# A selective-scan and window-attention kernel: counting who waits for a tile's room in the order's ranks, and taking two norms out of PSUM early

## The chip, the cores and the metric

The kernel runs on one core of a Trainium2 chip. The metric is the device time of one execution in microseconds (us). Five instruction queues are at work: PE (TensorE, matrix products), DVE (VectorE), ACT (ScalarE), POOL (GpSimd) and SP (SyncE, which here issues nearly all DMAs). Every queue works in order: an instruction that waits holds up all behind it on its engine.

## The reference

The input x is (8, 192, 64, 64), all in fp32. Two layers follow each other.

Layer 0 projects the 192 channels to 384, convolves each channel with a 3x3 kernel, and scans the image in four directions. For each direction and channel three gates Gl, Gm, Gr and the factors L, U, D come from a 16-wide projection of the pixel; the gates are divided by the sum of their absolute values. Columns are cut into chunks of 8, and in each chunk a step t does

```python
s = jnp.abs(Gl) + jnp.abs(Gm) + jnp.abs(Gr) + eps
hn = l * x + gl * h_up + gm * h + gr * h_dn      # h_up, h_dn: the rows above and below
out = out * Us + xs * Ds
```

The four directions are summed, normalised over channels, scaled by a global response norm per image, and projected back to 192 channels.

Layer 1 is a transformer block over windows of 8x8 pixels: a layer norm (the "first norm" here), q, k and v for six heads of 32, q and k brought to unit length, scores kept where they are among the 16 largest of a row, a softmax with a position bias, the product with v, a projection, a second norm, a GELU layer of width 768, and two residual sums. In the parts that matter here:

```python
shortcut = _layer_norm(xs, norm1_g, norm1_b)     # rsqrt(var + 1e-5) * g + b
attn = jnp.einsum('bhnd,bhmd->bhnm', _l2n(q), _l2n(k)) * temperature
```

## The kernel before

Three kinds of work are written down for each image b, as generators of steps.

`front` (line 490) does the first projection and the convolution and writes the result to DRAM twice, in the two orders in which the scans read it. `scan` (line 608) does the eight steps t. In each, for four directions and three blocks of 128 channels (12 tiles), PE makes the gates at line 673 into PSUM: two gates and L into three banks "g" and one bank "nb" (`gates`); later, for each pair of tiles, four more banks "g" with D and U (`both`). DVE, ACT and POOL do the rest: ab (L730, L761), pr (L737, L739, L776, L780, L791), rr (L772, L774), nb (L769, L787, L795), the new state hid (L802), and the output's parts dx and hu (L828, L833). `window_row` (line 1004) takes one row of eight windows (512 pixels, four tiles of 128 tokens) through all of layer 1: 64 rows in all.

PSUM has eight banks. Two are kept for "nb" (pool `n_ps`), and six are shared by everything else: pool `l_ps`, tag "lp", both for the "g" tiles of the scan and for the "lp" tiles of front, norms and windows (`bank()`, line 466). PE can't begin a tile before its bank has been read for the last time by whoever read the tile before.

In `window_row` the first norm goes like this. For each half t2 of the row, PE makes two token tiles of 192 columns side by side in one bank pz (L1047). The weights are centred, so the mean is zero already. ACT squares each from PSUM with an accumulated sum (L1053; the squares themselves land in the SBUF tile s0 and are overwritten later). POOL, ACT and POOL make the reciprocal root ss (`rsqrt`, L478 to L485). Then DVE multiplies the bank by ss and by the norm's gain n1_g into s0 (L1069), the last reader of pz. s0 is transposed by PE (L1012) and copied to sT (L1020).

For q and k, PE makes 384 columns in a bank pq (L1093), ACT copies them to the SBUF tile qk (L1101), then squares them in place in PSUM (L1108), and DVE sums the squares over each head (L1115), the last reader of pq. A reciprocal root follows, and DVE scales qk (L1166).

The order of the instructions on all queues is written by the program itself. Each step is given to `Plan` (line 78) with an engine, an assumed cost, its reads and writes, and a lane (steps of one lane that make tiles of one tag keep their order among themselves). A `Held` object is a tile that is to be made: the first step that uses it takes a slot of its pool, and the slot comes free when the last user has ended. `run` (line 170) plays the steps through: on each engine, of the steps that can start, it takes first those that need not wait longer than SLACK, and among them the one of the lowest rank. `order` (line 146) plays twelve times. The first time the ranks are those of the images; after each play, a step's rank becomes the latest time at which it could have started so that none of its successors would start later:

```python
for s in run:
    s.rank = min([d.start for d in s.after], default=s.end) - (s.end - s.start)
```

The shortest of the twelve plays is the order that is emitted. A step counts as successor only if it depends on the data or comes later on the same tile; a step that takes the slot which this one sets free isn't counted.

Of the kernel before, what the change touches and what calls it, by code (L numbers as in the profile page):

```python
# [25 lines left out]
AF = mybir.ActivationFunctionType  # L26
ALU = mybir.AluOpType
# [4 lines left out]
P = 128  # L32
# [22 lines left out]
class Held:  # L55


    def __init__(self, pool, shape, name, bufs=None, tag=None, dtype=F32):
        self.args = pool, shape, dtype, name, tag or name, bufs or pool.bufs
        self.tag, self.bufs = (id(pool), tag or name), bufs or pool.bufs  # L60
        self.users, self.left, self.end, self.tile = [], 0, 0.0, None

    def make(self):
        pool, shape, dtype, name, tag, bufs = self.args
# [13 lines left out]
class Plan:  # L78
# [67 lines left out]
    def order(self):  # L146

        before = [s.before for s in self.steps]
        tiles = {h: h.left for s in self.steps for h in s.held}
        best = None
        for _ in range(self.RUNS):
            for s, k in zip(self.steps, before):
                s.before, s.ready = k, 0.0
            for h, k in tiles.items():
                h.left, h.end = k, 0.0
            run = self.run()  # L160
            if best is None or self.length < best[0]:
                best = self.length, run, [s.start for s in run]
            for s in run:
                s.rank = min([d.start for d in s.after], default=s.end) - (s.end - s.start)
        self.length, run, starts = best
        for s, t in zip(run, starts):
            s.start = t
        return run

    def run(self):  # L170

        slots, queues = {}, {}
        counted, full = {}, {}
        done = []

        def clock(k):
            if k not in full:
                full[k] = counted.get(k - 1, 0.0) >= self.ENTRY
            return 2.4 if full[k] else 1.2

        def stream(t, cycles, share):
            while cycles > 1e-6:
                k = int(t / self.TICK)
                rate = clock(k)
                m = min(cycles, ((k + 1) * self.TICK - t) * rate + 1e-3)
                counted[k] = counted.get(k, 0.0) + m * share
                cycles -= m
                t += m / rate
            return t


        for s in self.steps:
            for h in s.makes:
                queues.setdefault((h.tag, s.lane), []).append(s)
                slots.setdefault(h.tag, [0.0] * h.bufs)
        first = {k: 0 for k in queues}

        def startable(s):

            t, need = s.ready, {}  # L200
            for h in s.makes:
                q = queues[h.tag, s.lane]
                if q[first[h.tag, s.lane]] is not s:
                    return None
                need[h.tag] = need.get(h.tag, 0) + 1
            for tag, n in need.items():
                kept = 0
                if s.lane and (tag, 0) in queues and first[tag, 0] < len(queues[tag, 0]):

                    f = queues[tag, 0][first[tag, 0]]  # L210
                    if not f.before and all(slots[h.tag] for h in f.makes if h.tag != tag):
                        kept = sum(h.tag == tag for h in f.makes)
                if len(slots[tag]) < n + kept:
                    return None
                t = max(t, sorted(slots[tag])[n + kept - 1])
            return t

        engines = sorted({s.engine for s in self.steps})
        pool = {e: [] for e in engines}
        dirty = set(engines)  # L220
        for s in self.steps:
            if not s.before:
                pool[s.engine].append(s)
        free = {e: 0.0 for e in engines}
        todo = len(self.steps)
        best = {e: None for e in engines}
        while todo:
            for e in dirty:
                pick = None
                for s in pool[e]:  # L230
                    t = startable(s)
                    if t is None:
                        continue
                    t = max(t, free[e])
                    late = max(0.0, t - free[e])
                    key = (late > self.SLACK, late if late > self.SLACK else 0.0, s.rank, s.n)
                    if pick is None or key < pick[0]:
                        pick = key, t, s
                best[e] = pick
            dirty = set()  # L240
            e = min((x for x in engines if best[x]), key=lambda x: best[x][1])
            _, t, s = best[e]
            s.start = t
            if e == "PE":
                cycles, share = s.cost
                end = stream(t + 60.0, cycles, share)
                free[e], s.end = end, end + 140.0
            else:
                hold, more = s.cost
                free[e] = t + hold  # L250
                s.end = free[e] + more
            pool[e].remove(s)
            dirty.add(e)
            todo -= 1
            done.append(s)
            for h in s.makes:
                first[h.tag, s.lane] += 1
                slots[h.tag].remove(min(slots[h.tag]))
            touched = bool(s.makes)
            for h in s.held:  # L260
                h.left -= 1
                h.end = max(h.end, s.end)
                if not h.left:
                    slots[h.tag].append(h.end + self.HOP)
                    touched = True
            if touched:
                dirty.update(engines)
            for d in s.after:
                d.before -= 1
                d.ready = max(d.ready, s.end + (self.HOP if d.engine != e else 30.0))  # L270
                if not d.before:
                    pool[d.engine].append(d)
                    dirty.update(engines)
        self.length = max(s.end for s in done)
        return sorted(done, key=lambda s: (s.start, s.n))
# [8 lines left out]
def tile_ss2d_then_window_attention(ctx: ExitStack, tc: tile.TileContext, a: dict, out: bass.AP):  # L284
# [719 lines left out]
    def window_row(b, g, z, sc, bb):  # L1004
# [31 lines left out]
        for t2 in range(2):  # L1036
            pz = bank()
            ss = Held(small, [P, 2], "ss")
            for k in range(2):

                def tokens(t2=t2, k=k, pz=pz):
                    tt = 2 * t2 + k
                    for ct in range(CT):
                        for w in range(2):
                            half = pz()[64 * w : 64 * w + 64, k * DM : (k + 1) * DM]
                            tok = view(zg(), [[CH, 64]], ct * 512 + 2 * tt + w)
                            nc.tensor.matmul(half, lhsT=tok, rhs=w_out[:, ct, :], start=ct == 0, stop=ct == CT - 1)  # L1047

                plan("PE", mm(3, DM), tokens, r=[zg], w=[(pz, k), (s0, "room")])
                plan(  # L1050
                    "ACT",
                    (430.0, 100.0),
                    lambda k=k, pz=pz, ss=ss, t2=t2: nc.scalar.activation(  # L1053
                        s0()[:, 2 * t2 + k, :], pz()[:, k * DM : (k + 1) * DM], AF.Square, accum_out=ss()[:, k : k + 1]
                    ),
                    r=[(pz, k)],
                    w=[(s0, t2), (ss, k)],
                )
            plan(
                "POOL",  # L1060
                tiny,
# [2 lines left out]
            )  # L1064
            rsqrt(ss, ss, [P, 2], "ss")

            def scaled(t2=t2, pz=pz, ss=ss):
                for k in range(2):
                    nc.vector.scalar_tensor_tensor(  # L1069
                        s0()[:, 2 * t2 + k, :],  # L1070
                        pz()[:, k * DM : (k + 1) * DM],
                        ss()[:, k : k + 1],
                        n1_g,
                        ALU.mult,
                        ALU.mult,
                    )

            plan("DVE", (650.0, 90.0), scaled, r=[pz, ss], w=[(s0, t2)])
            yield
        plan.lane = 7  # L1080
        two_blocks(sT, "sT", s0)
# [5 lines left out]
        for tt in range(NT):  # L1087
            pq = bank()

            def projected(tt=tt, pq=pq):  # L1090
                tok = slice(tt * P, (tt + 1) * P)
                for ci in range(2):
# [9 lines left out]
                r=[pq],  # L1102
                w=[(qk, tt)],
            )
            plan(
                "ACT",
                act(DIN),
                lambda pq=pq: nc.scalar.activation(pq()[:, 0:DIN], pq()[:, 0:DIN], AF.Square),  # L1108
                r=[(qk, tt)],
                w=[pq],  # L1110
            )
            plan(
                "DVE",
                vec(DIN),
                lambda tt=tt, pq=pq: nc.vector.tensor_reduce(  # L1115
                    nn()[:, tt, :], pq()[:, 0:DIN].rearrange("p (h d) -> p h d", d=HD), AX.X, ALU.add
                ),
                r=[pq],
                w=[(nn, tt)],
            )  # L1120
            yield
# [500 lines left out]
```

## Time and profile before

| what | value |
|---|---|
| median of 3 runs | 8548.28 us (8543.92 to 8550.57) |
| the profiled execution's own time | 8535.73 us |
| its span, first to last instruction | 8533.9 us |
| mean granted TensorE clock | 0.818 |
| PE matmuls ahead of the first window row's start (0 to 1180 us) | 844.7 us busy |
| rows beside scans (1180 to 7936 us) | 5728.3 us busy |
| rows alone after the last gate matmuls (7936 to 8534 us) | 493.2 us busy |

In the lines of the profile, L1069 is line 1069 of the kernel before. "out<-in" names the tiles written and read, and "32x512 f32" their partitions and elements. Busy time is the time in which the group had an instruction under way; mean is one instruction's own time, so neighbours that overlap have more mean than busy time. The idle time before a group is that of its engine, with what ended it: when that is the reader of a PSUM bank, and the group is a matmul whose inputs had long been there, the matmul waited for the bank's room. An fp32 matmul of the program appears as two in the profile in most forms. Idle time of an engine costs nothing where it isn't on the chain that ends last.

### The profile page before, as it was taken

The numbers are of one execution on the slowest core, as the hardware profiler recorded it, in microseconds if no ns is written. First come the engines' busy times: TensorE is split into PE (matmuls) and PEld (weight loads), VectorE is DVE, ScalarE is ACT, GpSimd is POOL, SyncE is SP. The second block draws the span as 40 slices with busy tenths as digits, with TensorE's granted clock in tenths as the row PEclk, the third lists the DMA queues.
The fourth block names the chain that finished last, engine by engine and source line by source line (L and its number), as shares of the span: only waits on it lengthen the run. The fifth ranks groups of instructions, "written<-read, shape, count | busy, mean of one in ns | idle before, by whom it ended". The sixth has DMA issues, their size and how long they took to land.

```text
span 8533.9 us, 147117 instructions
## 1 busy us (share of the span) xinstructions
PE 7066.1 (83%) x51224; PEld 3646.0 (43%) x51224; DVE 6350.5 (74%) x15549; ACT 5425.1 (64%) x12281; POOL 5839.1 (68%) x5918
## 2 busy tenths in 40 slices
PE   5787688888888888788888888888888888888887
PEld 2333344444444444444444444444444444444554
DVE  1366778888787887877788777787788888888543
ACT  1354447676676757665676656766577656667776
POOL 0377877778777677777777667676777777777311
PEclk8887578887888889786888888977778878778888
DMA  6776154212533155213531134311211111111110
GB/s 176 188 194 160 49 137 120 79 43 72 137 98 78 36 138 133 70 47 85 147 95 51 42 88 132 107 39 46 56 44 41 46 52 53 40 41 42 26 23 12
DMA packets 1037949, 695.69 MB, mean 82 GB/s; under 512 B 704116, under 2 KB 860215, under 8 KB 1037207
## 3 DMA queue, kind: packets, MB, share of 16 engines
q1 hardware_dynamic: 1035830, 684.99, 30.1%
q8 instruction: 406, 6.65, 0.3%
q14 instruction: 337, 2.75, 0.1%
q10 hardware_dynamic: 1376, 1.30, 0.1%
HBM read 453.43 MB, written 232.67 MB: 80 GB/s over the span
## 4 chain that ended last, share of the span: by engine, by line
PE 37%; DVE 17%; ACT 17%; POOL 13%; DMA 9%; issue 5%; SPq 1%; POOLq 0%; DVEq 0%; ACTq 0%
PE g L673 10%; PE lp L560 4%; PE lp L1477 4%; PE lp L1443 3%; POOL pr L791 3%; DMA strip<-pad 3%; DMA zg<-z 3%; ACT at L1276 2%; PE lp L1093 2%; PE lp L1047 2%; ACT at L1288 2%; POOL ab L761 2%; POOL pr L776 2%; POOL dx L842 2%; DVE pr L737 2%
## 5 line engine op out<-in xcount | busy, mean ns | idle before, releaser
L673 PE MATMUL g<-xe,w_g 32*128 32x512 f32 x3648 | 1301.1, 780 | 316.3 <-DVE dx L828 115.5
L673 PE MATMUL g<-xo,w_g 32*128 32x512 f32 x3648 | 1263.1, 774 | 238.5 <-DVE dx L828 65.1
L761 POOL TENSOR_TENSOR ab<-ab 128x512 f32<-128x512 f32 x672 | 863.2, 1285 | 407.3 <-ACT ab L730 401.4
L791 POOL TENSOR_TENSOR pr<-pr,rr 128x512 f32<-128x512 f32 x672 | 873.0, 1299 | 340.9 <-ACT rr L774 307.0
L776 POOL TENSOR_TENSOR pr<-pr 128x512 f32<-128x512 f32 x672 | 872.9, 1299 | 316.5 <-DVE pr L737 204.5
L730 ACT ACTIVATE ab<-g 128x512 f32<-128x512 f32 x1344 | 770.8, 593 | 320.6 <-PE nb L673 166.2
L560 PE MATMUL lp<-strip,w_cv 128*32 128x256 f32 x9216 | 687.2, 442 | 288.4 <-DMA strip<-pad 264.5
L780 POOL TENSOR_TENSOR pr<-pr 128x512 f32<-128x512 f32 x672 | 869.9, 1295 | 24.3
L842 POOL TENSOR_TENSOR dx<-dx,hu 128x512 f32<-128x512 f32 x576 | 739.0, 1291 | 183.6 <-DVE hu L833 172.3
L673 PEld LDWEIGHTS g<-xe,w_g 32*128 32x128 f32 x3648 | 461.1, 220 | 895.4 <-DVE dx L828 242.5
L673 PEld LDWEIGHTS g<-xo,w_g 32*128 32x128 f32 x3648 | 441.8, 219 | 804.5 <-issue 202.7
L772 ACT ACTIVATE rr<-nb,eps 128x512 f32<-128x512 f32 x672 | 460.0, 685 | 486.5 <-DVE nb L769 423.9
L787 DVE SCALAR_TENSOR_TENSOR nb<-nb,rr 128x512 f32<-128x512 f32 x672 | 465.2, 692 | 338.5 <-ACT rr L774 337.2
L1477 PE MATMUL lp<-hd,w_f 128*64 128x256 f32 (+1 forms) x2304 | 603.9, 500 | 75.2 <-ACT hd L1463 61.0
L795 DVE SCALAR_TENSOR_TENSOR nb<-nb,pr 128x512 f32<-128x512 f32 x672 | 464.8, 692 | 195.6 <-POOL pr L791 191.8
L560 PEld LDWEIGHTS lp<-strip,w_cv 128*32 128x32 f32 x9216 | 314.0, 123 | 669.3 <-issue 357.6
L850 POOL TENSOR_TENSOR y<-y,dx 128x512 f32<-128x512 f32 x384 | 596.4, 1561 | 3.1
L769 DVE TENSOR_TENSOR nb<-nb,ab 128x512 f32<-128x512 f32 x672 | 465.2, 692 | 154.9 <-POOL ab L761 125.8
L752 ACT ACTIVATE nb<-nb 128x512 f32<-128x512 f32 x672 | 396.8, 591 | 221.5 <-DVE pr L737 111.3
L840 POOL TENSOR_TENSOR y<-hu,dx 128x512 f32<-128x512 f32 x192 | 248.8, 1303 | 406.6 <-DVE hu L833 406.2
L833 DVE TENSOR_TENSOR hu<-g,hid 128x512 f32<-128x512 f32 x768 | 519.9, 678 | 8.0 <-PE g L673 6.4
L673 PE MATMUL nb<-xe,w_g 32*128 32x512 f32 x672 | 497.9, 829 | 8.0 <-DVE hid L802 7.9
(201 smaller groups left out, 17042.9 us busy)
## 6 DMA issues: line engine op xcount, KB each, us to landing
strip<-pad SPq DMA_DIRECT2D x1152, 132.0 KB
xd<-xsT SPq DMA_DIRECT2D x384, 256.0 KB
pad<-xin SPq DMA_DIRECT2D x192, 264.0 KB
xs<-st SPq DMA_DIRECT2D x192, 256.0 KB
xsT<-sn SPq DMA_DIRECT2D x192, 256.0 KB
xd<-xs SPq DMA_DIRECT2D x192, 256.0 KB
x<-xs SPq DMA_DIRECT2D x64, 768.0 KB
z<-y SPq DMA_DIRECT2D x64, 768.0 KB
```

What stands on the lines that cost most here:

```text
L560: nc.tensor.matmul(pc()[q * RG : (q + 1) * RG, k * 256 : (k + 1) * 256].rearrange("p (h w) -> p h w", h=4), lhsT=w_cv[:, ct, q, dx, :], rh ...
L673: nc.tensor.matmul(dst, lhsT=w[rows, col : col + P], rhs=xp[rows, :], start=True, stop=True)
L730: lambda r=r: nc.scalar.activation(ab()[:, r, :], g[r](), AF.Abs),
L761: plan("POOL", gp(512), lambda: nc.gpsimd.tensor_add(ab()[:, 0, :], ab()[:, 0, :], ab()[:, 1, :]), w=[ab])
L769: plan("DVE", vec(512), lambda: nc.vector.tensor_add(nb(), nb(), ab()[:, 0, :]), r=[ab], w=[nb])
L776: plan("POOL", gp(512), lambda: nc.gpsimd.tensor_add(one(), one(), pr()[:, 1, :]), r=[(pr, 1)], w=[(pr, 0)])
L780: lambda: nc.gpsimd.tensor_add(one(), one(), pr()[:, 2, :]),
L791: plan("POOL", gp(512), lambda: nc.gpsimd.tensor_mul(one(), one(), rr()), r=[rr], w=[(pr, 0)])
L833: lambda: nc.vector.tensor_mul(like(hu(), d), like(pu(), d), state(d, ct)),
L842: plan("POOL", gp(512), lambda: nc.gpsimd.tensor_add(dx(), dx(), hu()), r=[hu], w=[dx])
L850: nc.gpsimd.tensor_add(y, y, dx().rearrange("p (c i) -> p i c", c=CH))
L1477: nc.tensor.matmul(dst[:, at : at + rhs.shape[-1]], lhsT=lhsT, rhs=rhs, **flags)
```

## The change

It has three parts.

1. In the plan, a slot of a pool now remembers which tile it held. When a step takes the slot, the tile that held it notes this step as `next`. A step's rank is then also bounded by the start of the `next` of each tile that it uses. Among slots that are free equally early, the order in which they are taken is settled by a second number, no longer left open.
2. First norm: DVE multiplies both token tiles by the gain n1_g from pz into s0 in one instruction (line 1059 of the kernel after); ACT then squares pz in place, with the accumulated sums (1071), as pz's last reader; after the reciprocal root, ACT scales s0 in place in SBUF, two instructions (1085). The DVE instructions of L1069 are gone.
3. q and k: ACT's square goes from pq to a new SBUF tile sq, of which there is one (`bufs=1`), and DVE's reduce reads sq. The last reader of pq is now ACT, either by the square or by the copy, which no longer have an order between them.

```diff
 class Held:
-        self.users, self.left, self.end, self.tile = [], 0, 0.0, None
+        self.users, self.left, self.end, self.next, self.tile = [], 0, 0.0, None, None
...
 Plan.order:
-                h.left, h.end = k, 0.0
+                h.left, h.end, h.next = k, 0.0, None
...
-                s.rank = min([d.start for d in s.after], default=s.end) - (s.end - s.start)
+                needs = [d.start for d in s.after] + [h.next.start for h in s.held if h.next]
+                s.rank = min(needs, default=s.end) - (s.end - s.start)
...
 Plan.run:
-                slots.setdefault(h.tag, [0.0] * h.bufs)
+                slots.setdefault(h.tag, [(0.0, k, None) for k in range(h.bufs)])
...
-                t = max(t, sorted(slots[tag])[n + kept - 1])
+                t = max(t, sorted(slots[tag], key=lambda x: x[:2])[n + kept - 1][0])
...
-                slots[h.tag].remove(min(slots[h.tag]))
+                slot = min(slots[h.tag], key=lambda x: x[:2])
+                slots[h.tag].remove(slot)
+                if slot[2]:
+                    slot[2].next = s
...
-                    slots[h.tag].append(h.end + self.HOP)
+                    slots[h.tag].append((h.end + self.HOP, h.users[0].n + h.bufs, h))
...
 window_row, first norm:
-                plan(
-                    "ACT",
-                    (430.0, 100.0),
-                    lambda k=k, pz=pz, ss=ss, t2=t2: nc.scalar.activation(
-                        s0()[:, 2 * t2 + k, :], pz()[:, k * DM : (k + 1) * DM], AF.Square, accum_out=ss()[:, k : k + 1]
-                    ),
-                    r=[(pz, k)],
-                    w=[(s0, t2), (ss, k)],
-                )
+            two = slice(2 * t2, 2 * t2 + 2)
+            plan(
+                "DVE",
+                vec(2 * DM),
+                lambda two=two, pz=pz: nc.vector.tensor_mul(
+                    s0()[:, two, :],
+                    pz()[:, 0 : 2 * DM].rearrange("p (k m) -> p k m", k=2),
+                    n1_g.unsqueeze(1).to_broadcast([P, 2, DM]),
+                ),
+                r=[pz],
+                w=[(s0, t2)],
+            )
+
+            def squares(pz=pz, ss=ss):
+                for k in range(2):
+                    part = pz()[:, k * DM : (k + 1) * DM]
+                    nc.scalar.activation(part, part, AF.Square, accum_out=ss()[:, k : k + 1])
+
+            plan("ACT", (860.0, 100.0), squares, w=[pz, ss])
...
-            def scaled(t2=t2, pz=pz, ss=ss):
+            def scaled(t2=t2, ss=ss):
                 for k in range(2):
-                    nc.vector.scalar_tensor_tensor(
-                        s0()[:, 2 * t2 + k, :],
-                        pz()[:, k * DM : (k + 1) * DM],
-                        ss()[:, k : k + 1],
-                        n1_g,
-                        ALU.mult,
-                        ALU.mult,
-                    )
-
-            plan("DVE", (650.0, 90.0), scaled, r=[pz, ss], w=[(s0, t2)])
+                    part = s0()[:, 2 * t2 + k, :]
+                    nc.scalar.activation(part, part, AF.Copy, scale=ss()[:, k : k + 1])
+
+            plan("ACT", (600.0, 120.0), scaled, r=[ss], w=[(s0, t2)])
...
 window_row, q and k:
+            sq = Held(lpool, [P, DIN], "sq", bufs=1)
             plan(
                 "ACT",
                 act(DIN),
-                lambda pq=pq: nc.scalar.activation(pq()[:, 0:DIN], pq()[:, 0:DIN], AF.Square),
-                r=[(qk, tt)],
-                w=[pq],
+                lambda pq=pq, sq=sq: nc.scalar.activation(sq(), pq()[:, 0:DIN], AF.Square),
+                r=[pq],
+                w=[sq],
             )
             plan(
                 "DVE",
                 vec(DIN),
-                lambda tt=tt, pq=pq: nc.vector.tensor_reduce(
-                    nn()[:, tt, :], pq()[:, 0:DIN].rearrange("p (h d) -> p h d", d=HD), AX.X, ALU.add
+                lambda tt=tt, sq=sq: nc.vector.tensor_reduce(
+                    nn()[:, tt, :], sq().rearrange("p (h d) -> p h d", d=HD), AX.X, ALU.add
                 ),
-                r=[pq],
+                r=[sq],
                 w=[(nn, tt)],
             )
```

## The prediction

> **What bounds the kernel now.** I read the page's busy times first, then the span in its three stretches, then who waits for whom, then the groups of the lines that the change touches.
>
> The page's busy times and its chain by engine:
>
> ```profile
> span 8533.9 us, 147117 instructions
> PE 7066.1 (83%) x51224; PEld 3646.0 (43%) x51224; DVE 6350.5 (74%) x15549; ACT 5425.1 (64%) x12281; POOL 5839.1 (68%) x5918
> ...
> PE 37%; DVE 17%; ACT 17%; POOL 13%; DMA 9%; issue 5%; SPq 1%; POOLq 0%; DVEq 0%; ACTq 0%
> ```
>
> No engine is full, and the chain passes through all of them. The program ends when a mesh of short waits has been worked off. PE, the busiest, stands still for 8533.9 − 7066.1 = 1468 us.
>
> Busy times in three stretches: before the first window row, rows beside scans, rows alone (columns: stretch, length, then PE, PEld, DVE, ACT, POOL busy, TensorE clock, DMA share, GB/s):
>
> ```profile
> 0.00:1180.00 1180.00, 844.67 (x5910) 371.82 (x5910) 638.98 (x1029) 459.67 (x768) 675.94 (x541) 0.75 0.57 151
> 1180.00:7936.00 6756.00, 5728.25 (x41076) 2971.84 (x41076) 5451.20 (x13240) 4529.13 (x10355) 5053.40 (x5089) 0.82 0.28 75
> 7936.00:8534.00 598.00, 493.23 (x4242) 302.33 (x4238) 260.36 (x1281) 436.30 (x1160) 109.80 (x289) 0.88 0.09 20
> ```
>
> The middle decides: PE is 85% busy there and idle for 1028 us. The last 598 us hold window rows alone; PE is 82% busy, DVE 44%.
>
> The groups of the gate matmuls and of the two norms (columns: busy us, mean ns, idle time before and what ended it):
>
> ```profile
> L673 PE MATMUL g<-xe,w_g 32*128 32x512 f32 x3648 | 1301.1, 780 | 316.3 <-DVE dx L828 115.5 <-DVE lx L722 41.5 <-DMA xe<-flat 29.1
> L673 PE MATMUL g<-xo,w_g 32*128 32x512 f32 x3648 | 1263.1, 774 | 238.5 <-DVE dx L828 65.1 <-DVE lx L722 59.6 <-ACT ab L730 22.1
> L1053 ACT ACTIVATE s<-lp 128x192 f32<-128x192 f32 x256 | 83.1, 325 | 92.8 <-PE lp L1047 91.9
> L1069 DVE SCALAR_TENSOR_TENSOR s<-lp,ss,n_g 128x192 f32<-128x192 f32 x256 | 92.1, 407 | 38.0 <-POOL ss L485 37.7
> L1108 ACT ACTIVATE lp<-lp 128x384 f32<-128x384 f32 x256 | 125.1, 492 | 0.0
> L1115 DVE TENSOR_REDUCE nn<-lp 128x12 f32<-128x384 f32 x256 | 138.7, 548 | 131.5 <-ACT lp L1108 130.8
> ```
>
> PE idles 316.3 + 238.5 = 555 us ahead of gate matmuls, mostly until DVE or ACT has read something. Their only inputs are xe and xo, so a DVE or ACT release means that one of six PSUM banks came free: a third of PE's idle time is want of a bank.
>
> Who holds banks too long? Pairing the squares L1053 and scalings L1069 in the timeline, 128 pairs, a bank of the first norm lies dead from the end of its second square to the end of its scaling for 14.75 us on average (median 12.6, ninth decile 28.9), 1887 us in all. PE's idle time ahead of gate matmuls overlaps these dead times by 118.6 us. For q and k, from the end of the square L1108 to the end of the reduce L1115, it is 2.76 us (median 1.05).
>
> **What the skill says.** The Trainium skill, "Perfetto Trace Analysis", Optimization Strategy: the same gap repeating on the engine that should be saturated can mean that PSUM lacks room for the next tile. The trace agrees (555 us before gate matmuls). The same page, Optimizing Scalar/DVE Operations, says that moving work to Scalar may help where DVE is saturated; here DVE is at 81% of the middle, ACT at 67%, so that reason is weak.
>
> **The change, part by part.**
>
> *First norm.* Removed: the DVE scaling, 128 pairs, 92.1 us busy. Added: 128 DVE products of 384 columns out of PSUM; L1368 has this shape and takes 547 ns (69.8 us for 128), so 70 us. DVE: −22 us. The squares stay on ACT, now PSUM to PSUM; L1108 (492 ns) against the copy L1101 of the same size into SBUF (481 ns) says 11 ns more, 256 × 11 = +3 us. Added on ACT: 256 copies of 192 columns in SBUF with a scale pointer. The trace has no such shape. The skill, "ScalarE: Activation LUTs", What ACT_TABLE_LOAD costs, prices an activation with one pointer at 280 ns + 0.833 ns a column, and lets neighbours overlap by 93 ns: 440 ns each, 787 a pair, 128 × 787 = +101 us (estimate). The trace agrees with the page: L1276 (64 columns, one pointer) takes 338 ns against 333. Upper end L1411 with two pointers, 125 us; lower end L1053's 83 us.
>
> *q and k.* The square goes to SBUF (481 for 492 ns, −3 us). The reduce reads SBUF: L1281 takes 678 ns for 512 columns in SBUF, L1115 548 for 384 in PSUM, 1.02 ns a column more, so no change. No DMA is added or moved in the norms.
>
> What this work weighs: ACT carries 17% of the chain at 64% busy, 0.27 of its time; DVE 17/74 = 0.23. ACT +101 × 0.27 = **+27 us** (0 if all hides behind the 33% of the middle that ACT is idle, +101 without that cover); DVE −22 × 0.23 = **−5 us** (−22 to 0).
>
> *Banks.* The bank of the first norm is now held over a DVE product and two squares, not over the reciprocal root. I take what that gives from the built order of the instructions, which shows each tile's bank: between the first write of a first-norm bank and the next tile's first write there, PE streams 14,640 columns before and 9,326 after. At 8533.9 us for 6,276,264 columns (1.36 ns each) that is 7.2 us less, 49% of the 14.75 dead ones. For q and k the distance rises, 5,996 to 6,538: no gain. Of 118.6 us overlap 49% is 58 us. Of the columns won (128 × 5,314 = 680,000) the gate banks get 377,000, 55%; the rest goes to the convolution and to q and k. So 58 × 0.55 = 32 to 58: I take **−45 us**. Ends: 0 (a gate step needs four banks, and one more may not start it) and −119.
>
> *Ranks.* They issue nothing; they reorder every queue, SP's and POOL's included. The order shows one thing plainly: after the last gate matmul 367,875 columns are left before and 337,411 after, 8.3% less, nearly one window row. At the stretch's own rate that is 598 × 0.083 = 50 us that move ahead of the end of the scans. If the middle takes them in at its present 85% nothing is won (30,464 columns cost as much there); if they fit into PE's idle time, all 50. The banks make that room and are partly counted, so I take half: **−25 us** (−50 to +60; the loss, were steps that free room to go ahead of chain steps, would be one late microsecond at each of the 64 scan steps).
>
> Sum against the profiled execution's 8535.7 us: −45 − 25 + 27 − 5 = −48, 8488. The median of the runs, 8548.3, lies 12.6 above that execution; so 8500, −0.56%.
>
> **New waits.** The squares of the first norm now wait for the DVE product; behind them on ACT stand gate work (ab, rr) and window copies, for which DVE and POOL wait (ab L761 waits 401 us for ACT already). In exchange the scaling of s0, for which only the transposes L1012 wait, is a median 18 ACT instructions behind the squares, some 18 × 0.44 = 8 us (5425.1 us over 12,281 instructions), no later than the present 14.75.
>
> **Rivals.**
>
> *A, slower: the single buffer for the squares of q and k.* ACT's next square must now stand until DVE's reduce has read the last one; a bank each hid this before. In the present timeline 51 of the 256 squares start before the previous reduce has ended, by 198 us together. If ACT stands there that long, 198 × 0.27 = +53, giving 8553; at full weight, +198, 8698. For: the reduce starts over 2 us after its square in 62 of 256 cases. Against: the order sets squares further apart (a median of 14 ACT instructions for 9). It decides from 241 us of standing: 241 × 0.27 = 65 turns −48 into +17. Taken with the ranks' loss end it would be about 8600.
>
> *B, no change.* The freed bank goes to tiles on which PE doesn't wait, and ACT's +27 eats the rest: −32 + 27 − 5 = −10, 8538. For: conv banks go from 14,575 to 15,237 columns. Against: the shorter last stretch.
>
> *C, much faster.* The whole overlap is won (−119), and the whole moved row (−50), less 22 net of ACT and DVE: −147, 8401. For: with a denser PE the clock granted (0.82 in the middle, 0.88 at the end) may rise. Against: bank distance of the gates grows by only 1.2%, 7,091 to 7,178 columns.
>
> *D, the ranks do nothing or harm alone.* Then −23 stays, 8525.
>
> **How the numbers follow.** A difference under 0.2% (17 us) can't be told from none. Likeliest (8445 to 8531, D in it) 0.53; C, below 8445, 0.13; B, within 0.2%, 0.13; A and the ranks' loss, above 8565, 0.21. Faster 0.66, same 0.13, slower 0.21. The range 8415 to 8600 leaves out about 0.08 of C and 0.09 of A; the likeliest case's own range is 8445 to 8531.
>
> **What would show it.** Right: dead time of first-norm banks well under 14.75 us; PE idle before gate matmuls falls from 555 by 40 or more; ACT busy +90 to +110, DVE −20; the stretch after the last gates falls from 598 to about 550 us. Wrong: a large wait of ACT's square for DVE's reduce, or of the first-norm squares for the DVE product; or gate idle unchanged, with more idle ahead of other lines; or a middle stretch that lengthens by more than the tail shrinks.

## The result: 2.9% faster

The changed kernel takes 8296.85 us (8293.42 to 8306.46, 4 runs), the kernel before 8546.1 us in the same comparison: a ratio of 0.9711 (95% interval 0.9694 to 0.9728), 249 us less. I forecast the right side, but 46 us, a fifth of it, and the time lies below my range.

The page of the kernel after, busy times:

```profile
span 8292.0 us, 147108 instructions
PE 6951.0 (84%) x51224; PEld 3600.7 (43%) x51224; DVE 6381.9 (77%) x15421; ACT 5488.0 (66%) x12537; POOL 5859.7 (71%) x5918
```

PE's 51,224 matmul records are busy for 115 us less (7066.1 before), and PE is idle for 127 us less (1341 for 1468); together that is the 242 us by which the profiled span fell. The first half is not less work: the same matmuls ran, under a granted clock of 0.827 for 0.818 on average. In proportion to the clock that makes 77 of the 115 us (my estimate: 7066 x (1 - 0.818/0.827)). What raised the clock wasn't tested, and it isn't needed for a gain: e1 below has a span 80 us shorter than before at a clock of 0.815.

The three stretches of the kernel after (columns as in the prediction):

```profile
0.00:1190.00 1190.00, 832.55 (x5886) 376.75 (x5886) 640.76 (x1028) 458.31 (x767) 675.47 (x541) 0.74 0.56 150
1190.00:7752.00 6562.00, 5680.32 (x41464) 2951.28 (x41464) 5503.76 (x13245) 4621.40 (x10678) 5090.75 (x5108) 0.84 0.29 77
7752.00:8292.00 540.00, 438.12 (x3874) 272.69 (x3874) 237.38 (x1149) 408.33 (x1094) 93.51 (x269) 0.90 0.10 22
```

The last stretch fell from 598 to 540 us, as the order had promised (about 550). But the middle, which took that row in, did not stay as long as it was: it fell from 6756 to 6562. DVE's idle time there fell from 1305 to 1058 us, PE's from 1028 to 882; PE stayed the fullest (87% busy, DVE 84%).

The groups of the kernel after that answer to those shown before (busy us, mean ns, idle before and what ended it):

```profile
L678 PE MATMUL g<-xe,w_g 32*128 32x512 f32 x3648 | 1281.3, 777 | 284.0 <-DVE dx L833 90.3 <-DMA xe<-flat 29.2 <-ACT sq L1118 27.5
L678 PE MATMUL g<-xo,w_g 32*128 32x512 f32 x3648 | 1218.2, 767 | 270.1 <-DVE dx L833 154.0 <-DVE lx L727 23.4 <-ACT lp L1071 12.3
L1118 ACT ACTIVATE sq<-lp 128x384 f32<-128x384 f32 x256 | 126.5, 494 | 39.5 <-PE lp L1102 26.6 <-DVE nn L1125 12.5
L1085 ACT ACTIVATE s<-s,ss 128x192 f32<-128x192 f32 x256 | 101.1, 449 | 19.1 <-POOL ss L490 18.8
L1071 ACT ACTIVATE lp<-lp 128x192 f32<-128x192 f32 x256 | 81.6, 319 | 29.4 <-DVE s L1059 24.8
L1059 DVE TENSOR_TENSOR s<-lp,n_g 128x384 f32<-128x384 f32 x128 | 69.9, 548 | 53.4 <-PE lp L1052 53.3
```

The prices of the single operations were right: the product takes 548 ns (I took 547) and 69.9 us, the scaling on ACT 101.1 us (101). The engines' totals were not: ACT rose by 63 us (5488.0 for 5425.1), not by 90 or more, and DVE rose by 31 in place of falling by 20 (the last section says why). Added group by group, ACT's times rose by 111 us; the rest went into overlap of neighbouring instructions.

The idle time before gate matmuls, which I took as the place where the gain would be seen, is 554 us, as before (555). That equality is in part an accident of this order: in three kernels below that gain about as much it is 513 (e7), 516 (e8) and 509 us (e9). What does hold is that the wait for a first-norm bank itself was small. Before the change, the trace puts only 7.5 us of the 555 down to the first norm's scaling and 26.4 to the sums of q and k:

```profile
  PE g L673: 7.5, 9
PE g L673 <- DVE nn L1115: 26.4, 12, 6.0
```

(The first line is from the list of who waited for L1069: us, times; the second adds the longest.) The 118.6 us by which I saw dead banks and idle time overlap were mostly waits for other readers, above all dx and lx, which read banks of the gates themselves (40 and 39 us). The 127 us that PE idles less lie mostly before matmuls of the window rows; the largest piece, 42 us, is before the transposes of the attention.

To see the banks themselves I matched each PSUM tile of the built program with its instructions in the trace and summed, over all tiles of a kind, the time from PE's first write to the last reader's end ("taken"), the part of it in which nobody works on the tile ("dead"; PE counts as working from its first write to its last), and the time from the last reader's end to the next tile's first write ("empty"). The last tile of each bank is left out.

| us of bank time, taken / dead / empty | before | e1, ranks only | e4, both norms | after |
|---|---|---|---|---|
| first norm (128 tiles) | 2614 / 1905 / 287 | 2757 / 2024 / 210 | 1069 / 452 / 240 | 1182 / 567 / 243 |
| q and k (256) | 1859 / 1034 / 630 | 2149 / 1327 / 570 | 2463 / 1786 / 546 | 2286 / 1616 / 504 |
| gates and outputs (4318) | 32014 / 21365 / 10667 | 32188 / 21466 / 10021 | 32465 / 21733 / 10712 | 32179 / 21586 / 10185 |
| all eight banks | 47144 / 27228 / 18846 | 47605 / 27606 / 17755 | 46732 / 26974 / 18354 | 46457 / 26702 / 17709 |

A first-norm bank is taken for 9.2 us, not 20.4 (1182/128, 2614/128), and lies dead for 4.4. Other tiles took up half of what it gave. Those of q and k above all waited longer for their readers: from PE's end to the first read 2.8 us on average, for 1.2 before.

### The profile page after: what moved, and what is told of

Its sections match the earlier page's. It is cut to its first block, busy times and chain, and to the rows that moved or that the text cites. A ratio compares the mean times of both kernels' runs of the same rounds, so it can differ in the third digit from the quotient of the medians.

```text
span 8292.0 us, 147108 instructions
## 1 busy us (share of the span) xinstructions
PE 6951.0 (84%) x51224; PEld 3600.7 (43%) x51224; DVE 6381.9 (77%) x15421; ACT 5488.0 (66%) x12537; POOL 5859.7 (71%) x5918
## 4 chain that ended last, share of the span: by engine, by line
PE 23%; ACT 15%; DVE 14%; POOL 9%; DMA 5%; issue 4%; SPq 0%; POOLq 0%; DVEq 0%; ACTq 0%
PE g L678 6%; PE lp L1487 3%; PE lp L1453 2%; ACT at L1286 2%; ACT at L1298 2%; DMA zg<-z 2%; POOL pr L796 2%; PE lp L1052 2%; PE lp L565 2%; DVE pr L742 1%; PE lp L1102 1%; POOL pr L781 1%; ACT ab L735 1%; DMA strip<-pad 1%; POOL ab L766 1%
## 5 line engine op out<-in xcount | busy, mean ns | idle before, releaser
L678 PE MATMUL g<-xe,w_g 32*128 32x512 f32 x3648 | 1281.3, 777 | 284.0 <-DVE dx L833 90.3
L678 PE MATMUL g<-xo,w_g 32*128 32x512 f32 x3648 | 1218.2, 767 | 270.1 <-DVE dx L833 154.0
L781 POOL TENSOR_TENSOR pr<-pr 128x512 f32<-128x512 f32 x672 | 887.2, 1321 | 339.7 <-DVE pr L742 254.8
L785 POOL TENSOR_TENSOR pr<-pr 128x512 f32<-128x512 f32 x672 | 884.2, 1316 | 20.6
L678 PEld LDWEIGHTS g<-xo,w_g 32*128 32x128 f32 x3648 | 423.4, 217 | 812.4 <-DVE dx L833 278.4
```

Of the source, the lines that this page charges most:

```text
L678: nc.tensor.matmul(dst, lhsT=w[rows, col : col + P], rhs=xp[rows, :], start=True, stop=True)
L781: plan("POOL", gp(512), lambda: nc.gpsimd.tensor_add(one(), one(), pr()[:, 1, :]), r=[(pr, 1)], w=[(pr, 0)])
L785: lambda: nc.gpsimd.tensor_add(one(), one(), pr()[:, 2, :]),
```

## The experiments

Four theories: **banks** (the early end of the norms' banks paid), **ranks** (the new order paid whatever the norms do), **chance** (any new order moves the time), and, from the middle stretch of the kernel after, **DVE** (its work sets the middle, with far more weight than I gave it). Times are medians; the ratio is to the kernel before, with its 95% interval.

### Each part alone, and both norms under the old ranks

e1 applies only the planner's part of the diff, e2 only the first norm's, e3 only that of q and k, e4 the last two.

> Only the ranks count who waits for a tile's room (with the slots' tie order); both norms as before. Theory 'banks' (the early end of the first norm's bank is what paid): within 0.5% of before, 8505 to 8590. Theory 'ranks' (the new order paid, whatever the norms do): at least two thirds of the 249 us, so under 8380. Theory 'order by chance' (any new order moves the time by a per cent or two): anything from 8350 to 8650, and then kernels with meaningless changes of the plan spread as widely.

> Only the first norm is rewritten (bank freed after a DVE product and two squares, scaling on ACT in SBUF); ranks and q, k as before. Theory 'banks': at least two thirds of the gain, under 8380, with the idle time of PE and DVE down. Theory 'ranks': 8500 to 8560, as my prediction has it for banks and ACT's work together (-45 + 27 - 5).

> Only the squares of q and k go to SBUF. Theory 'banks': a part of the gain, -30 to -80, since each of 256 banks ends some 2 to 3 us earlier. Prediction's view: no gain (0, or up to +53 if ACT stands for the reduce).

> Both norms rewritten, ranks as before. Theory 'banks': nearly the whole gain, 8290 to 8350. Theory 'ranks': 8480 to 8560. If the parts only pay together, this lies between, and e1 too is short of its share.

| | time | ratio |
|---|---|---|
| e1, ranks | 8450.67 | 0.9885 (0.9871 to 0.9900) |
| e2, first norm | 8487.96 | 0.9930 (0.9913 to 0.9946) |
| e3, q and k | 8567.96 | 1.0022 (1.0009 to 1.0036) |
| e4, both norms | 8422.57 | 0.9856 (0.9841 to 0.9871) |

No single theory holds. Ranks give 1.15%, both norms 1.44%, together 2.6 of the 2.9%. The first norm alone gives 60 us (0.70% of 8546), between "ranks" and "banks". q and k alone lose a little; on top of the first norm they win 0.74%. How much of such differences can be the luck of an order is measured in the next part.

The middle and last stretches of e1:

```profile
1195.00:7860.00 6665.00, 5739.81 (x41072) 2969.43 (x41072) 5478.97 (x13238) 4514.68 (x10348) 5070.03 (x5085) 0.82 0.28 76
7860.00:8453.00 593.00, 492.84 (x4270) 303.86 (x4266) 261.70 (x1286) 439.40 (x1168) 108.92 (x293) 0.88 0.09 20
```

The ranks alone shorten the middle by 91 us with the same work in it (41,072 matmul records for 41,076). They move no row out of the last stretch, which stays at 593 us for 598, though that row was what I had priced. In the table above they shorten no bank's hold; the time for which banks stand empty falls by 1091 us of bank time. That follows from a shorter span with the same holds, so it names no cause.

### Is it chance?

The planner is a greedy play with ties and near-ties, so a meaningless change of the assumed costs gives another order:

```diff
+        cost = (cost[0] + len(self.steps) % 4, cost[1])
         s = Step(engine, fn, cost, self.rank, self.lane, len(self.steps))
```

e5 and e6 do this to the kernel before (modulo 4 and 7), e7 and e8 to the changed one.

> A control for chance: the kernel before with each step's assumed cost raised by its number modulo 4 (0 to 3 ns, or cycles on PE), which means nothing and only makes the plan fall into another order. Theory 'order by chance': differs from before by 1% or more either way. Theories 'banks' and 'ranks': within 0.5% of before, 8500 to 8590.

> The same with the number modulo 7. 'Order by chance': another value, 1% or more from before or from the other jitter. Otherwise within 0.5% of before.

> The changed kernel with the meaningless jitter modulo 4. 'Order by chance': the changed kernel's gain of 2.9% was partly luck, and this loses a third of it or more (over 8380). Otherwise within 0.5% of the changed kernel, 8255 to 8340.

> The changed kernel with the jitter modulo 7: same two expectations, over 8380 or 8255 to 8340.

Before: 8568.86 (ratio 1.0035, 1.0019 to 1.0051) and 8552.34 (1.0018, 1.0007 to 1.0029). After: 8263.53 (0.9684, 0.9669 to 0.9698) and 8338.79 (0.9769, 0.9754 to 0.9784). A redrawn order moved the kernel before by up to 0.35% and the changed one by up to 0.6%, and the two redraws of the changed one lie 0.9% apart. So the 2.9% is no luck, and e1 (1.15%) and e4 (1.44%) are beyond it. The first norm alone (0.7%) and the 0.74% that q and k add to it are not clear of it, and e3's loss means nothing. Three orders of each kernel are few, so 0.9% is a lower bound on what chance can do. Each later experiment also redraws the order; those on the changed kernel are best set against the slowest of its three orders, e8 with 0.9769, and the fastest, e7 with 0.9684.

### Whose room do the ranks count?

```diff
-                needs = [d.start for d in s.after] + [h.next.start for h in s.held if h.next]
+                needs = [d.start for d in s.after] + [h.next.start for h in s.held if h.next and h.args[4] in ("lp", "nb")]
```

e9 is this, in the changed kernel; e10 has "not in"; e16 is e9's line in the kernel before with its old norms.

> The changed kernel, but a step's rank counts who waits for room only where the room is a PSUM bank (tags lp and nb). If the ranks pay through the banks: the changed kernel's time, 8264 to 8339 (the spread of the jittered ones). If they pay through the rooms of SBUF and DRAM tiles: near e4 with both norms and the old ranks, 8390 to 8450.

> The mirror image: room counts for all tiles except PSUM banks. Through the banks: 8390 to 8450. Through the rest: 8264 to 8339. If both e9 and e10 gain half, both kinds of room matter.

> The kernel before with ranks that count who waits for PSUM banks only, norms as they were. If the ranks pay through the banks whatever the norms do: as e1, 8420 to 8470. If the banks' ranks need the early ends of the two norms' banks: 8500 to 8560.

e9: 8283.38 us, 0.9697 (0.9676 to 0.9718), the full gain. e10: 8368.17, 0.9800 (0.9779 to 0.9820); against e4's 0.9856 the other rooms alone, with the slots' new tie order, give 0.6%, no more than chance can, and its interval also touches e8's. e16: 8494.39, 0.9940 (0.9917 to 0.9963), half of e1 and between its two expectations; its distance from e1 (0.55%) is within chance, so it decides nothing. In the changed kernel it suffices that the ranks count who waits for a PSUM bank.

### The banks held again

In e11 ACT reads one column of the first norm's bank after the scaling, in e17 one column of the bank of q and k after DVE's reduce. The rest of the work stays, and the banks end late.

```diff
 e11, in scaled, and pz in its reads:
+                nc.scalar.copy(look, pz()[:, 0:1])
 e17, a step of its own:
+                lambda tt=tt, pq=pq: nc.scalar.activation(
+                    look, pq()[:, 0:1], AF.Identity, bias=nn()[:, tt, 0:1]
+                ),
+                r=[pq, (nn, tt)],
```

> The changed kernel, with one more ACT instruction after the scaling that reads a single column of the first norm's bank, so that the bank stays taken until then (128 x 0.2 us of ACT more, 7 us at the weight 0.27). Theory 'banks': the first norm's share is lost again, 60 to 130 us: 8350 to 8430. If the first norm's share came from the engines' loads: 8264 to 8346.

> The changed kernel, with one more ACT instruction for each tile of q and k, after DVE's reduce, that reads one column of the bank: the bank is taken until the sum is made, as before the change. ACT gets 256 x 0.29 = 74 us more, +31 at the weight of e12 (0.42). If the q and k part paid 104 us (e13) through the earlier end of its banks: +100 to +135, 8395 to 8430. If it paid through something else (the freed order of copy and square, the reduce's source): about +31, 8300 to 8360.

> The changed kernel without the q and k part (ranks and first norm only). If that part pays once the banks are what the order turns on: 60 to 100 us slower than the changed kernel, 8355 to 8400. If it pays nothing, as it did alone (e3) and as I predicted: 8264 to 8339, the spread of the jittered kernels.

e11: 8362.09, 0.9788 (0.9763 to 0.9814), 65 us lost against the changed kernel, of which the extra ACT reads (18.4 us busy) explain little. Its first-norm banks are taken for 2522 us, for 1182. But its interval overlaps that of e8, so the loss is not told from chance. e17: 8400.01, 0.9843 (0.9828 to 0.9857), 1.3% lost (103 us between the medians, 113 by the ratios), with some 28 for ACT's 67 us of extra reads by e12's weight; its banks of q and k are taken for 3185 us, for 2286. e13, the changed kernel without the q and k part, is as slow: 8400.55, 0.9827 (0.9809 to 0.9845). Both are clear of e8. The waits of gate matmuls for the last reader of these banks point the same way (e11, e13, e17; us, times, longest):

```profile
PE g L679 <- ACT look L1087: 49.2, 20, 8.2
PE g L678 <- DVE nn L1124: 59.0, 23, 8.1
PE g L679 <- ACT look L1135: 103.7, 35, 17.2
```

In the changed kernel it is 21.9 us for the first norm's squares, and 47.9 for the square and the copy of q and k. So the early end of the q and k banks, which I had at zero, is worth having beside the other two parts. That of the first norm's banks is likely worth something, but e2 and e11 don't show it beyond chance. e17 has a side effect that wasn't parted: POOL, which next writes the sums in place, must wait for the added read. It idled 172.9 us for it, for 140.8 us for DVE's reduce in the changed kernel, a small difference. e17's last stretch:

```profile
7795.00:8409.00 614.00, 482.06 (x4116) 295.88 (x4116) 254.78 (x1250) 450.58 (x1223) 100.83 (x288) 0.86 0.09 20
```

It is 614 us, for 540: rows fall behind the scans and are left for the end. That is how slower versions show here in general, not a mark of held banks: it is 636 us in e14 below.

### What ACT's and DVE's work weighs

```diff
 e12, before each scaling on ACT:
+                    nc.scalar.activation(part, part, AF.Copy, scale=one[:, 0:1])
 e14, a step on DVE after the product out of the bank:
+                    s0()[:, two, :], s0()[:, two, :], one.unsqueeze(2).to_broadcast([P, 2, DM])
 e15, the scaling on DVE:
-                    nc.scalar.activation(part, part, AF.Copy, scale=ss()[:, k : k + 1])
+                    nc.vector.tensor_scalar(part, part, ss()[:, k : k + 1], None, ALU.mult)
```

> The changed kernel with each ACT scaling preceded by a scaling with one, of the same shape: ACT busy +101 us. The weight that my prediction gave to ACT's work (0.27) says +27 us, 8324 within the spread; a full weight +101, 8398; no weight 8297.

> The changed kernel with a second DVE product of the same shape, s0 times one in SBUF, after the one out of the bank: DVE busy +70 us, no bank held longer. Theory 'DVE is the bound of the middle once banks come free': weight near 1, 8350 to 8380. The weight of my prediction, 0.23: +16, within the spread, 8264 to 8345.

> The changed kernel with the scaling of s0 in SBUF on DVE and not on ACT: ACT busy -101, DVE some +80; the bank ends as early as before. 'DVE is the bound': slower, +30 to +60, 8330 to 8360. If ACT's work weighs more than DVE's (e12 gave 42 for 101 us): faster, 8240 to 8280.

e12: 8339.08, 0.9765 (0.9746 to 0.9784): 42 us for the ACT work, a weight of 0.4, but within chance, so it may be nothing. e14: 8414.78, 0.9850 (0.9830 to 0.9870): 118 us, clear of e8. e15: 8491.67, 0.9935 (0.9918 to 0.9951): 195 us, nearly four fifths of the whole gain given back by the choice of the engine on which 256 small products run. The delay that e14 adds to a row can't be the reason alone: e12 delays the same tile s0 by as much.

The groups on s0 in e14 (the added product and the one out of the bank), then in e15 (scaling, product):

```profile
L1072 DVE TENSOR_TENSOR s<-s,one 128x384 f32<-128x384 f32 x128 | 112.4, 886 | 0.8
L1060 DVE TENSOR_TENSOR s<-lp,n_g 128x384 f32<-128x384 f32 x128 | 69.8, 550 | 65.8 <-PE lp L1053 65.4
```

```profile
L1085 DVE TENSOR_SCALAR s<-s,ss 128x192 f32<-128x192 f32 x256 | 190.4, 789 | 62.9 <-POOL ss L490 62.8
L1059 DVE TENSOR_TENSOR s<-lp,n_g 128x384 f32<-128x384 f32 x128 | 70.1, 550 | 91.9 <-PE lp L1052 91.1
```

The added DVE work was dearer than I had expected (112 us for 70, 190 for 80). Per busy microsecond of its group DVE weighs 118/112 = 1.05 in e14; in e15, with ACT's relief of 101 at 0.42 added back, (195 + 42)/190 = 1.25. These are rough: chance is some 50 to 75 us, and DVE's total rose by less than the groups' time (by 76 us in e14, 6458.0 for 6381.9). That DVE's work weighs far more than my 0.23 is safe. In e14 the loss shows at the end:

```profile
1190.00:7767.00 6577.00, 5669.34 (x41220) 2934.34 (x41220) 5550.05 (x13272) 4585.83 (x10575) 5098.24 (x5090) 0.83 0.28 77
7767.00:8403.00 636.00, 488.81 (x4122) 299.70 (x4118) 266.77 (x1251) 448.44 (x1197) 103.02 (x288) 0.85 0.08 19
```

The middle is only 15 us longer than in the changed kernel, but it holds 244 matmul records less, which stand in the last stretch.

### Less work for DVE: a version that beats both

In e18 ACT copies the first norm's bank to s0 and squares it, and POOL multiplies s0 by the gain in SBUF, in place of DVE's product:

```diff
-                lambda two=two, pz=pz: nc.vector.tensor_mul(
-                    s0()[:, two, :],
-                    pz()[:, 0 : 2 * DM].rearrange("p (k m) -> p k m", k=2),
-                    n1_g.unsqueeze(1).to_broadcast([P, 2, DM]),
-                ),
+                lambda two=two, pz=pz: nc.scalar.copy(
+                    s0()[:, two, :].rearrange("p k m -> p (k m)"), pz()[:, 0 : 2 * DM]
+                ),
...
+                lambda two=two: nc.gpsimd.tensor_mul(
+                    s0()[:, two, :], s0()[:, two, :], n1_g.unsqueeze(1).to_broadcast([P, 2, DM])
+                ),
```

> A version that may beat both: the changed kernel with the first norm's bank copied to s0 by ACT and the product with the gain made by POOL in SBUF. DVE busy -70, ACT some +58, POOL some +125. If DVE's work weighs about 1 as in e14 and e15, and POOL's little: -70 + 24 = -46, 8250. If POOL's weighs as much as DVE's: +80, 8375.

8203.72 us, 0.9612 (0.9596 to 0.9628): 93 us faster than the changed kernel between the medians, 85 by the ratios, and 0.7% below the fastest of that kernel's three orders. It has no redrawn orders of its own. Its busy times and the moved groups:

```profile
PE 6908.7 (84%) x51224; PEld 3585.0 (44%) x51224; DVE 6355.7 (78%) x15293; ACT 5525.2 (67%) x12665; POOL 6003.9 (73%) x6046
```

```profile
L1068 POOL TENSOR_TENSOR s<-s,n_g 128x384 f32<-128x384 f32 x128 | 131.8, 1031 | 23.8 <-ACT s L1059 23.5
L1059 ACT COPY s<-lp 128x384 f32<-128x384 f32 x128 | 60.9, 476 | 27.8 <-PE lp L1052 27.2
```

DVE loses 69.9 us of products, ACT gains 61 of copies and POOL 132, and the time falls by no less than the DVE part. The bank also no longer waits for DVE (747 us taken, for 1182), and this run doesn't part the two.

## Why the prediction was wrong

Step by step, measured as ratios of the before kernel's 8546 us:

- **First norm.** Predicted −45 (banks) + 27 (ACT) − 5 (DVE) = −23; alone it gave −60 (e2). The banks do end early, as I said. With ACT at 0.42 (+42) and DVE's 22 us at about 1 (−22) the banks' term is some −80 from e2; e11 puts it at 57 from the other side. Both are uncertain by the 50 us or more of a redrawn order, so that the early end paid is supported and not shown. Two sizes were wrong: the saving (7.2 us a bank from the column distance; the trace says 20.4 − 9.2 = 11.2), and a weight of DVE read from its share of the chain (0.23) that measured about 1. And the wait from which I priced it, 118.6 us of overlap, was not a wait for these banks: the trace puts 7.5 us down to them.
- **q and k: "the distance rises, no gain".** This step failed outright. Predicted 0; taken out of the changed kernel it costs 1.16%, 99 us (e13), and holding the banks to the reduce costs 1.3%, some 75 to 85 us without ACT's extra reads (e17). The distance between two tiles' first writes isn't the time for which a bank must be held. In the new order PE starts these tiles sooner before their readers (2.8 us for 1.2), and the distance rises although each bank is free 3.5 us earlier than in e17 ((3185 − 2286)/256). Alone the part gave nothing (e3). That it pays beside the other two parts is measured; which of them it needs, and why, is open.
- **Ranks: "I take half: −25".** Predicted −25, with −50 as the end of its range; alone they gave −98 (e1), on top of both norms 124 (0.9856 to 0.9711). I took the row that left the last stretch as the measure of the new order, and took the middle's density as given. This step failed, and that its sign came out was luck: the ranks alone moved no row (593 for 598 in e1) and took 91 us out of the middle. With all parts the row left (598 to 540), which is 58 us, and the middle shrank by 194 with more in it. An order shows what moved past the end of a stretch, but not how long each engine will stand idle inside it.
- **Where it would show.** I looked for bank waits in PE's idle time before gate matmuls. It stayed (555, 554), and fell by some 40 in e7 to e9. The rest of PE's gain was spread over the waits of the rows' matmuls and over less busy time at a higher granted clock (0.82 to 0.84 in the middle). A rising clock I had only in rival C, as the effect of a denser PE; the stretches don't support that reason by themselves, since the last one of the kernel before had 0.88 with PE 82% busy, the middle 0.82 with 85%. C's time was 8401, and even that was too high by 104. Of my signs, the dead time of first-norm banks (4.4 us) and the last stretch (540) came as said; gate idle, ACT's and DVE's totals did not.
- **Rival A, the single buffer sq**, fell. The page's groups show ACT's square waiting 12.5 us in all for DVE's reduce (L1118, "DVE nn"), not the 198 us read off the old timeline; the new order is planned with the single buffer in it. The other new wait, first-norm squares for the product, is 24.8 us.

What stays open: by which steps the ranks shorten the middle. In e1 the banks aren't held for less time, and no run here shows which waits the new order saved. The sum of all parts is shown, and so is that ranks and norms each carry more than chance; how the gain divides among them is known to about 50 us.

## What to carry to other kernels

When six banks are shared by a scan and by several side stages, price a bank by how long its last reader makes it wait, on every stage that uses it, and test that by holding it again with a one-column read; look also at whom the trace names as the end of PE's waits, since an overlap in time is not yet a wait. Don't weigh an engine's work by its share of the chain that ended last: DVE, the second fullest engine of the middle, counted about in full, as far as chance lets one say, though it idled a sixth of the time; and in e18 work taken from it, with the bank's still earlier end, was worth more than larger pieces given to ACT and POOL. In a kernel whose order is planned, redraw the order with meaningless costs first, since here differences under 0.9% couldn't be told from the draw.

## What I had not expected of the hardware

Some DVE instructions that read and write only SBUF took far longer beside POOL's work, and one that reads PSUM did not. The product out of PSUM took 524 to 559 ns (median 547) in the kernel after; the same product out of SBUF in e14, by the trace's durations of its line:

```profile
L1072 DVE TENSOR_TENSOR s<-s,one x128: 508/706/1665, 1197.1 to 8271.4; 128x384 f32<-128x384 f32 x128
```

(shortest, median and longest in ns), and the scaling of 192 columns in e15 269, 700 and 1664 ns. The Trainium skill, "Perfetto Trace Analysis", Optimizing Scalar/DVE Operations, says that GPSIMD and DVE share an SBUF read port; the traces agree. I split the instructions by whether POOL had one of its own under way (those only partly beside one are left out):

| median ns (count) | no POOL instruction at the time | POOL at work throughout |
|---|---|---|
| e14, added product, SBUF only | 552 (14) | 976 (68) |
| e15, scaling, SBUF only | 312 (52) | 1315 (101) |
| kernel after, product out of PSUM | 549 (15) | 547 (73) |
| predicated copy of the mask, before | 734 (95) | 1683 (33) |
| the same, after | 735 (54) | 1689 (68) |

The predicated copy in SBUF, which the change doesn't touch, went from 988 to 1227 ns on average. The table shows why: it is no slower in itself, but more of it falls beside POOL's work in the denser middle. The split holds within the middle stretch alone too: 546 and 976 ns for the added product of e14, 736 and 1689 for the copy after the change.

```profile
L1261 DVE COPY_PREDICATED at<-less,neg 128x512 f32<-128x512 uint8 x192 | 235.5, 1227 | 6.6
```

The predicated copy's group grew by 46 us (235.5 for 189.7), and that of the comparison before it by 24. So DVE was busy 31 us more after the change (6381.9 for 6350.5), though 22 us of its work had left.
